# Second norm's rows turned through DRAM, and the linear steps of each window put in another order, in an adaLN transformer block

## The chip, the cores and the metric

The kernel runs on 1 core of one Trainium2 chip, in one launch. The metric is the device time of a run in microseconds (us); less is better. The time of the kernel before is the median of 3 runs.

## The reference

One transformer block with adaptive layer norm (adaLN), on x of 8 batches, 1024 tokens and 512 channels in float32, 16 heads of 32 channels, and an MLP of 2048 hidden channels. Cut to what matters:

```python
mod = silu(condition) @ Wada + bada
sh_a, sc_a, gt_a, sh_m, sc_m, gt_m = split(mod, 6, axis=1)
xn = layernorm(x, g1, be1)                        # over the 512 channels
xm = xn * (1 + sc_a) + sh_a
q, k, v = split_heads(xm @ Wqkv)                  # 16 heads of 32
attn = softmax(causal(q @ k.T * 32 ** -0.5))
x = x + gt_a * ((attn @ v) @ Wproj + bproj)
xn = layernorm(x, g2, be2)                        # the second norm
xm = xn * (1 + sc_m) + sh_m
h = gelu_exact(xm @ W1 + b1)
x = x + gt_m * (h @ W2 + b2)
```

## The kernel before

**Tiles.** The 8 x 1024 tokens are cut into NB = 16 blocks of TB = 512 tokens: `blocks[n]` is (batch, half), so an even n is the first half of a batch and an odd n the second, whose attention also reads the first half's keys and values. P is 128, and a block is four row tiles of 128 tokens by 512 channels (tokens on partitions) or, turned, four chunks of 128 channels by 512 tokens. All matmuls are float32 and split into four tiles of 32 columns (or 32 rows) of the array that run side by side: one call of the helper `matmul` (L201, its instruction is L205) issues four instructions, and the profile counts two records for each of them, so 8 records a call.

**Linear steps.** k, q, v, the attention's projection ("proj"), the four parts of the up matmul ("u") and the down matmul (four parts "d", 7 products in all) are done by Strassen's scheme: 7 products of half-size operands instead of 8. A product of k, q, v, proj or u is 4 calls of `matmul`; a product of d is 16. The operands B11, B21, B22, T1 to T4 are halves of the turned rows (`xm_m`, `xm_a`) and sums of halves (`t_m`, `t_a`), made in `modulated` (L732). Products go to one of three PSUM banks (`banks`), and are combined from there by VectorE (L197) or copied by either VectorE or ScalarE (L189, L192).

**The norms and how rows are turned.** The first norm ("a", of x) and the second ("m", of the residual after the attention) work on rows: statistics (L628) on VectorE, scaling (L653) on ScalarE. Then the rows must be turned so that channels lie on partitions. There are two ways in the kernel. By TensorE: 16 transposes of 128 x 128 a block into PSUM (L769), and the modulation reads PSUM (L778 or L784). Through DRAM (`turn_rows`, L702): VectorE transposes 32 x 32 squares (L708, four instructions a block), four DMAs write them to a DRAM tile ("put", L719), and one DMA reads the turned block back ("get", L725); the modulation then reads and writes SBUF. `is_turned(key)` (L377) picks the way: in the kernel before, DRAM for the first norm of blocks 4 to 15, and TensorE for all others and for every second norm. For the first norm the rows of x are loaded in such an order that the turned columns come out in the order of the tokens.

**The order of the work.** The kernel is laid out by a planner that runs when the program is built. `plan[w]` lists the linear steps of window w; the attention of block w is woven in between. `now` holds a modelled clock for each engine, `due` when an operand is counted as written, and the linear step or the attention's unit that is counted as ready first is written next; what comes out is a fixed order of instructions on each engine. Three lists are worked off beside it: `jobs` (statistics and turns, on VectorE), `pool_jobs`, and `transfers` (the puts and gets). Every DMA but four is issued on SyncE's queue (SP), in the fixed order. Weights come through a ring of 9 tiles (`fetch`, L336); a tile is loaded again when TensorE has used it.

In window w of the kernel before (n = w - 1) the steps are: what is left of the older up and down parts, v(w), the load of the residual's rows (`load_xr`), proj(n), k(w + 1), the second norm's turning `mt`, q(w + 1), up parts, and then down parts of n. The residual of a block (`xr`) has one buffer, block 14 has a buffer of the keys' pool (`kT`, three buffers). The results are stored (L1193) as soon as their last sum has been written into the program. The token half operands of the second norm are contiguous slices: `"B11": xm[:, one, left_half]`.

Of the kernel before, what the change touches and what calls it, by code (L numbers as in the profile page):

```python
# [22 lines left out]
def kernel(  # L23
# [72 lines left out]
    shape = [None]  # L96
    pool_spans = []
    NEVER = float("inf")
# [13 lines left out]
    def note(engine, ns, reads=(), writes=(), port=False):  # L112
        start = max(now[engine], due(reads, writes))
        if port:
            start = max([start] + [b for a, b in pool_spans if a <= start < b])
        end = start + ns
        now[engine] = end
        if engine == "POOL":
            pool_spans.append((start, end))
            del pool_spans[:-16]  # L120
# [80 lines left out]
    def matmul(ps, lhsT, rhs, start, stop, reads=(), bank=None):  # L201

        for j in range(HPG):
            r = slice(j * hd, (j + 1) * hd)
            nc.tensor.matmul(  # L205
                ps[r, :], lhsT[:, r], rhs, start=start, stop=stop, skip_group_check=True
            )
        n = 1
        for d in rhs.shape[1:]:
            n *= d  # L210
        note_pe(2 * COLUMN * n, "columns", reads, [] if bank is None else [("l", bank)])

    MM = 853
# [26 lines left out]
    }  # L240
    late = []
    for w in range(1, NB):
        n = w - 1
        m = mlp_steps(n)
        even = blocks[n][1] == 0
        rows_a = [("rows", blocks[n][0], "a")] if even else []
        rows_m = [("rows", blocks[n][0], "m")] if even else []
        own = m[:1] + ([("load_xa", w + 2)] if w + 2 < NB else []) + m[1:3]
        own += [("norm_a", w + 2)] if w + 2 < NB else []
        if w == NB - 1:  # L250
            steps = late[:1] + [("load_xr", n)] + rows_a + [("proj", n), ("mt", n)] + late[1:]
            steps += [("v", w)] + rows_m + own + m[3:6]
            late = m[6:]
        else:
# [5 lines left out]
            at = [("at", w + 2)] if w + 2 < NB else []  # L260
            if blocks[w][1] == 0:

                late = m[3:4] + at + m[4:]
            else:
                steps += m[3:4] + at + m[4:6]
                late = m[6:]
        plan[w] = steps
    n = NB - 1
    plan[NB] = [("load_xr", n), late[0], ("beside", ("proj", n)), late[1], ("mt", n)] + mlp_steps(n)

# [103 lines left out]

    SQ = 32

    def is_turned(key):  # L377
        return key[0] == "a" and int(key[1:]) >= 4

# [181 lines left out]

    def add_job(job, reads, first=False):

        at = sum(1 for other in jobs if other[2]) if first else len(jobs)
        jobs.insert(at, (job, reads, first))

    def run_jobs(everything=False):
        while jobs and (
            everything or (now["DVE"] <= now["PE"] and due(jobs[0][1]) <= now["PE"])
        ):  # L570
            jobs.pop(0)[0]()

    transfers = []

    def run_transfers(everything=False):
        while transfers and (
            everything or max(queue_free[0], transfers[0][0]) <= now["PE"]
        ):
# [28 lines left out]
    def hurry():  # L607

        while jobs and due(jobs[0][1]) <= now["PE"] + 500:
            jobs.pop(0)[0]()  # L610
        while excursions and due(excursions[0][1]) <= now["PE"] + 500:
            excursions.pop(0)[0]()
# [4 lines left out]
    def normalize(tiles, key, sources):  # L617
# [42 lines left out]
        for t in range(NTT):  # L660
            add_job(lambda t=t: statistics(t), [sources[t]], key[0] == "m")

# [39 lines left out]
    def turn_rows(key, tiles, xm):  # L702

        squares = xm.rearrange("p c (j r) -> p (c j) r", r=P)
        there = kept.tile([D, TB], F32, tag=f"turned_{int(key[1:]) % 2}", name=f"turned_{key}")

        def turn(t):
            nc.vector.transpose(  # L708
                squares[:, :, ts(t, SQ)], tiles[t].rearrange("p (k r) -> p k r", r=SQ)
            )  # L710
# [18 lines left out]
        for t in range(NTT):  # L729
            add_job(lambda t=t: turn(t), [("hat", key, t)])  # L730
# [82 lines left out]
    qTs, kTs, vs = {}, {}, {}  # L813
    projected, valued = set(), set()
    xm_of, hTs, hidden = {}, {}, set()
# [80 lines left out]
    def strassen(step, x, dest, target, row, done, put=None, after={}):  # L896
# [14 lines left out]
        def product(a, t, bank=None):  # L911
            start = bank is None
            reads = [(x, t)] + ([("sums", *step, a)] if raw and a[0] == "S" else [])
            for i in range(2):
                for k in range(2):
# [10 lines left out]
                    lhsT, rhs = (second, first) if row else (first, second)  # L926
                    matmul(
                        banks[bank][:, ts(i, HB)], lhsT[:, ts(i, P)], rhs,
                        start and i + k == 0, k == 1, reads, bank,
# [59 lines left out]
        start(tail())  # L989

    def project_T(step, store, pool, tag, done):

        n = step[1]
        dst = pool.tile([P, NC, TB], F32, tag=tag, name=f"{tag}_{n}")
        store[n] = dst
# [27 lines left out]

    residual, stored = {}, {}
    y_count, y_keys = [0], {}
# [69 lines left out]
    def project_out(n):  # L1095
# [8 lines left out]
        begun = []  # L1104

        def begin(t):

            bank = yield from accumulate(
                [(attT[:, c, ts(t, P)], piece(at[c])) for c in range(NC - 1)], [("att", n)], False
            )  # L1110
            begun.append(bank)

        for t, xt in enumerate(tiles):
            if last:
                while len(begun) <= max(t, 1):
# [3 lines left out]
                matmul(  # L1119
                    banks[bank], attT[:, NC - 1, ts(t, P)], piece(at[NC - 1]), False, True,  # L1120
                    [("att", n, t)], bank,
                )
            else:
                bank = yield from accumulate(
                    [(attT[:, c, ts(t, P)], piece(at[c])) for c in range(NC)], [("att", n)]
                )
# [62 lines left out]
    def store(n, t):  # L1189
        b, h = blocks[n]  # L1190
        for i in (2 * t, 2 * t + 1):
            r0 = h * TB + i * P
            nc.sync.dma_start(out[b, r0 : r0 + P, :], residual[n][:, i, :])  # L1193
        stored[n + 1] = max(stored.get(n + 1, 0.0), due([("xr", n, 2 * t), ("xr", n, 2 * t + 1)]))

    def down(n, part):
# [19 lines left out]
        def product(operand):  # L1216
# [3 lines left out]
            for i in range(NQ):  # L1220
                p = next(at)
                for k in range(2):
                    c = 2 * i + k
                    hT = hTs[n, 2 * kh + c // NC][:, c % NC, tokens]
                    for m in range(2):
# [3 lines left out]
                        else:  # L1229
                            yield [], []  # L1230
                        matmul(
                            banks[bank][:, ts(m, HB)], hT[:, ts(m, P)], halves(p)[:, k, :],
                            c + m == 0, c == 2 * NQ - 1, reads, bank,
# [96 lines left out]
    def perform(step):  # L1330
# [12 lines left out]
        elif kind == "load_xr":  # L1343
            n = step[1]
            b, h = blocks[n]
            if n == NB - 2:
                xr = kvp.tile([P, NTT, D], F32, tag="kT", name=f"xr_{n}")
            else:
                xr = xrp.tile([P, NTT, D], F32, tag="xr", name=f"xr_{n}")
            residual[n] = xr  # L1350
            for t in range(NTT):
                r0 = h * TB + t * P
                nc.sync.dma_start(xr[:, t, :], x[b, r0 : r0 + P, :])
                landed = max(now["PE"], stored.get(n, 0.0)) + LANDING + 700 * t
                written["xr", n, t] = landed
# [15 lines left out]
        elif kind == "k":  # L1371
            yield [("free for k", step[1])], []
            yield from project_T(step, kTs, kvp, "kT", lambda: None)
        elif kind == "q":
# [449 lines left out]
    def attend():  # L1824
        previous = None
        for n in range(NB):
# [20 lines left out]
            written["free for k", n + 2 if n % 2 else n + 1] = 0.0  # L1847
            written["free for k", n + 1] = 0.0
            for g, k, n_slots, upto in slots:
                if (n, g) == groups[-1]:  # L1850
# [50 lines left out]
    def next_scores():  # L1901
        until(lambda: units[unit_at[0]][0] in projected)
        scores(*units[unit_at[0]])
# [15 lines left out]
    needs += sum(score_need(*unit) for unit in units)  # L1919
    for n in range(NB):  # L1920
        written["attended", n] = NEVER
        written["v done", n] = NEVER
# [30 lines left out]
    run_jobs(True)  # L1953
    drain()


# [46 lines left out]
```

## Time and profile before

| what | kernel before |
|---|---|
| median of 3 runs | 3485.6 us (3483.39 to 3485.79) |
| profiled execution, its own time | 3487.44 us |
| its span in the profile | 3485.7 us |
| TensorE (PE) busy | 3448.3 us, 99% |
| VectorE (DVE), ScalarE (ACT), GpSimd (POOL) busy | 1905.0, 1286.7 and 2074.5 us |
| DMA | 466.84 MB, mean 134 GB/s |
| clock granted to TensorE | full speed |

How to read it: busy is the time in which an engine has an instruction; idle time of an engine that is not the bottleneck costs nothing. The profiled execution's own time is 1.7 us longer than its span (launch and end), and 1.8 us longer than the median of the runs. Lines such as L205 are lines of the kernel before; they move by some tens of lines in the changed kernel.

### The profile page before, as it was taken

The numbers are of one execution on the slowest core, as the hardware profiler recorded it, in microseconds if no ns is written. First come the engines' busy times: TensorE is split into PE (matmuls) and PEld (weight loads), VectorE is DVE, ScalarE is ACT, GpSimd is POOL, SyncE is SP. The second block draws the span as 40 slices with busy tenths as digits, with TensorE's granted clock in tenths as the row PEclk, the third lists the DMA queues.
The fourth block names the chain that finished last, engine by engine and source line by source line (L and its number), as shares of the span: only waits on it lengthen the run. The fifth ranks groups of instructions, "written<-read, shape, count | busy, mean of one in ns | idle before, by whom it ended". The sixth has DMA issues, their size and how long they took to land.

```text
span 3485.7 us, 122756 instructions
## 1 busy us (share of the span) xinstructions
PE 3448.3 (99%) x55618; PEld 1776.1 (51%) x55618; DVE 1905.0 (55%) x2136; ACT 1286.7 (37%) x1420; POOL 2074.5 (60%) x2209
## 2 busy tenths in 40 slices
PE   8999999999999999999999999999999999999999
PEld 5544455445554554545545455454554545545445
DVE  6765664554645556465564655645546455554463
ACT  2335243352433524235152352514524244241531
POOL 3676755675466664576645766557664576644640
PEclk9999999999999999999999999999999999999999
DMA  6843334335353353633536335363443534435334
GB/s 213 271 144 86 117 110 150 120 105 172 107 167 102 105 174 104 186 95 100 173 98 186 98 111 159 101 186 98 129 140 101 183 101 135 130 100 153 90 121 136
DMA packets 350523, 466.84 MB, mean 134 GB/s; under 512 B 27460, under 2 KB 212092, under 8 KB 350004
## 3 DMA queue, kind: packets, MB, share of 16 engines
q1 hardware_dynamic: 349808, 458.73, 43.8%
q8 instruction: 438, 7.18, 0.9%
q14 instruction: 81, 0.66, 0.1%
q10 hardware_dynamic: 196, 0.28, 0.0%
HBM read 416.90 MB, written 41.99 MB: 132 GB/s over the span
## 4 chain that ended last, share of the span: by engine, by line
PE 94%; DVE 3%; POOL 1%; ACT 1%; issue 0%; DMA 0%; SPq 0%; DVEq 0%; ACTq 0%; POOLq 0%
PE bank L205 65%; PE sc L1602 9%; PE po L1736 8%; PE st L1695 7%; PE st L1683 3%; DVE mx L1619 2%; PE bank L1757 2%; PE bank L769 1%; PE bank L1657 1%; POOL pT L1821 0%; DVE sc L1616 0%; POOL mcols L1640 0%; DVE pT L1818 0%; POOL mcols L1641 0%; DMA ada<-in_L_cond_Wada_dram 0%
## 5 line engine op out<-in xcount | busy, mean ns | idle before, releaser
L1821 POOL TENSOR_TENSOR pT<-pT,pT 128x256 f32<-128x256 f32 (+3 forms) x1254 | 1174.5, 972 | 210.3 <-ACT pT L1708 119.2
L1708 ACT ACTIVATE pT<-st 128x2048 f32<-128x2048 f32 x288 | 541.1, 1879 | 1001.1 <-PE st L1695 908.8
L205 PE MATMUL bank<-w,hT 128*32 128x256 f32 x14336 | 795.5, 379 | 0.0
L1619 DVE TENSOR_REDUCE mx<-sc 128x4 f32<-128x2048 f32 (+3 forms) x384 | 665.6, 1754 | 140.3 <-PE sc L1602 133.7
L205 PEld LDWEIGHTS bank<-w,hT 128*32 128x32 f32 x14336 | 448.8, 110 | 335.6 <-issue 29.2
L205 PE MATMUL bank<-xm_m,w 128*32 128x256 f32 x8192 | 498.8, 380 | 0.0
L205 PE MATMUL bank<-t_m,w 128*32 128x256 f32 x6144 | 384.2, 380 | 0.1
L205 PEld LDWEIGHTS bank<-xm_m,w 128*32 128x32 f32 x8192 | 253.6, 110 | 238.8 <-issue 76.0
L1713 POOL TENSOR_SCALAR_AFFINE_SELECT pT<-pT 128x512 f32<-128x512 f32 x256 | 164.8, 661 | 308.8 <-ACT pT L1708 306.9
L1602 PE MATMUL sc<-kT,qT 32*128 32x512 f32 (+3 forms) x3072 | 329.1, 520 | 2.9 <-DVE mx L1619 1.9
L1616 DVE TENSOR_TENSOR sc<-sc,mask 128x1024 f32<-128x1024 f32 (+1 forms) x160 | 162.9, 1018 | 276.2 <-PE sc L1602 217.6
L1736 PE MATMUL po<-pT,v 128*32 128x512 f32 (+3 forms) x3072 | 306.0, 493 | 0.0
L1695 PE MATMUL st<-qT,kT 32*128 32x512 f32 (+3 forms) x3072 | 299.8, 486 | 0.0
L205 PEld LDWEIGHTS bank<-t_m,w 128*32 128x32 f32 x6144 | 193.0, 110 | 180.8 <-issue 54.2
L205 PE MATMUL bank<-xm_a,w 128*32 128x256 f32 x3968 | 248.8, 381 | 1.3 <-ACT xm_a L784 1.1
L197 DVE TENSOR_TENSOR hT<-bank,u_u 128x512 f32<-128x512 f32 x192 | 129.1, 686 | 151.2 <-PE bank L205 149.0
L165 POOL TENSOR_TENSOR qT<-top,rec 128x512 f32<-128x512 f32 x60 | 77.1, 1285 | 219.8 <-ACT rec L1775 219.8
L1602 PEld LDWEIGHTS sc<-kT,qT 32*128 32x128 f32 x3072 | 129.4, 183 | 150.9 <-ACT pT L1708 61.8
L205 PE MATMUL bank<-w,qT 128*32 128x256 f32 (+1 forms) x2944 | 191.4, 399 | 1.3 <-DVE qT L1782 1.3
L1153 ACT ACTIVATE hT<-hT,cols 128x512 f32<-128x512 f32 x256 | 164.2, 711 | 55.0 <-DVE hT L197 54.4
L205 PE MATMUL bank<-t_a,w 128*32 128x256 f32 x2944 | 183.3, 380 | 0.0
L165 POOL TENSOR_TENSOR hT<-hT,hT 128x1024 f32<-128x1024 f32 x28 | 79.7, 2868 | 167.6 <-DVE hT L1211 167.6
(232 smaller groups left out, 3507.5 us busy)
## 6 DMA issues: line engine op xcount, KB each, us to landing
w<-in_L_cond_W_dram SPq DMA_DIRECT2D x384, 256.0 KB, 2.9
w<-kept_up_S SPq DMA_DIRECT2D x256, 256.0 KB, 2.6
w<-kept_down_S SPq DMA_DIRECT2D x256, 256.0 KB, 2.8
w<-kept_qkv_S SPq DMA_DIRECT2D x180, 256.0 KB, 2.7
w<-in_L_cond_Wqkv_dram SPq DMA_DIRECT2D x147, 256.0 KB, 3.0
hat<-in_x_dram SPq DMA_DIRECT2D x64, 256.0 KB, 4.7
xr<-in_x_dram SPq DMA_DIRECT2D x64, 256.0 KB, 4.6
out_dram<-xr SPq DMA_DIRECT2D x64, 256.0 KB, 2.6
```

Source lines behind the costliest of these rows:

```text
L165: nc.gpsimd.tensor_tensor(out, a, b, op)
L197: nc.vector.tensor_tensor(out, src, other, op)
L205: nc.tensor.matmul(ps[r, :], lhsT[:, r], rhs, start=start, stop=stop, skip_group_check=True)
L1153: nc.scalar.activation(hT[:, i, :], hT[:, i, :], AF.Gelu, bias=cols[:, O_B1 + f : O_B1 + f + 1])
L1602: nc.tensor.matmul(sc[:, j, c0 : c0 + w], qTs[n][r, gg, ts(qt, P)], keys_of(n, kh)[r, gg, :w], start=True, stop=True, skip_group_check=True,)
L1616: nc.vector.tensor_tensor(place, place, shape_of.to_broadcast(place.shape), ALU.add)
L1619: nc.vector.tensor_reduce(maxima[n, gg][:, kh, qt, :], sc[:, :, c0 : c0 + w], axis=AX.X, op=ALU.max)
L1695: nc.tensor.matmul(st[:, j, c0 : c0 + w], kT[r, gg, ts(k % NTT, P)], qT[r, gg, TB - w :], start=False, stop=True, skip_group_check=True,)
L1708: nc.scalar.activation(pT[:, :, :used], st[:, :, :used], AF.Exp, scale=scale)
L1713: nc.gpsimd.affine_select(diagonal, diagonal, pattern=[[0, HPG], [1, P]], compare_op=ALU.is_ge, fill=0.0, base=0, channel_multiplier=-1,)
L1736: nc.tensor.matmul(po[r, TB - w :], v[:, k % NTT, g * P + j * hd : g * P + (j + 1) * hd], pT[:, j, c0 : c0 + w], start=(k == 0), stop=last ...
L1821: nc.gpsimd.tensor_tensor(into, into, pT[:, j, c0 : c0 + w], ALU.add)
```

## The change

The second norm of blocks 3 to 13 is turned through DRAM, too. For these blocks the residual's rows are loaded, and the results stored, in a permuted order of rows; the turned columns are then in an order in which the token halves are four runs of 64, and `modulated` takes B11, T1, B21 and B22 as strided views. The steps of a window are ordered anew: older up parts, the residual's load, v, proj, `mt`, the four down parts of the block before, q, k, and then the up parts. So a block's down parts run a window later than its up parts, and two residuals are held at a time: odd blocks take a buffer of the keys' pool. Stores become `transfers`, which are issued at the modelled time at which they are counted as ready, as gets are (7000 ns after the last put's issue instead of 5000 ns after the turn). `jobs` are taken in any order across norms. The model now also lets a GpSimd instruction wait for VectorE's use of the shared port.

```diff
     def matmul(ps, lhsT, rhs, start, stop, reads=(), bank=None):
+        if len(rhs.shape) == 3:
+            ps = ps.rearrange("p (a n) -> p a n", a=rhs.shape[1])
...
+    def token_tile(columns, i, n):
+        if is_turned(f"m{n}"):
+            return columns.rearrange("p (a t r) -> p t a r", t=2, r=SQ)[:, i]
+        return columns[:, ts(i, P)]
+    def row_tiles_of(rows, n):
+        if is_turned(f"m{n}"):
+            tiles = rows.rearrange("(h a t r) d -> h t a r d", h=2, t=2, r=SQ)
+            return [tiles[i // 2, i % 2] for i in range(NTT)]
+        return [rows[ts(i, P), :] for i in range(NTT)]
...
-            steps = late + [("v", w), ("load_xr", n)] + rows_a + [("proj", n), ("k", w + 1)]
-            if w == 1:
-                steps = [("load_xr", n)] + rows_a + [("k", w + 1), ("proj", n)]
-            steps += [("mt", n), ("q", w + 1)] + rows_m + own
+        head = rows_a + [("load_xr", n)]
+        if w == 1:
+            steps = head + [("k", w + 1), ("proj", n), ("mt", n), ("q", w + 1)]
+        elif w == 2:
+            steps = downs[2:] + [("v", w)] + head + [("proj", n), ("mt", n), ("q", w + 1), ("k", w + 1)]
+        elif w < NB - 1:
+            steps = late + head + [("v", w), ("proj", n), ("mt", n)] + downs + [("q", w + 1), ("k", w + 1)]
+        else:
+            steps = late + head + [("v", w), ("proj", n), ("mt", n)] + downs
+        cut = m[2] if blocks[w][1] == 0 else None
+        i = ups.index(cut) if cut in ups else len(ups)
+        plan[w] = steps + rows_m + ups[:i]
+        late, downs = ups[i:], m[4:]
...
     def is_turned(key):
-        return key[0] == "a" and int(key[1:]) >= 4
+        n = int(key[1:])
+        return n >= 4 if key[0] == "a" else 3 <= n < NB - 2
...
+    def next_job(by):
+        passed = set()
+        for i, (_, reads, line, _) in enumerate(jobs):
+            if line not in passed and due(reads) <= by:
+                return i
+            passed.add(line)
+        return None
...
     def run_transfers(everything=False):
-        while transfers and (
-            everything or max(queue_free[0], transfers[0][0]) <= now["PE"]
-        ):
-            ready, transfer = transfers.pop(0)
+        while transfers:
+            i = min(range(len(transfers)), key=lambda i: transfers[i][0])
+            if not everything and max(queue_free[0], transfers[i][0]) > now["PE"]:
+                return
+            ready, transfer = transfers.pop(i)
             queue_free[0] = max(queue_free[0], now["PE"], ready) + 700
             transfer()
...
                 for a in range(P // SQ):
                     transfers.append((ready, lambda a=a: put(a)))
-                transfers.append((ready + 5000, get))
         def put(a):
+            if a == P // SQ - 1:
+                transfers.append((queue_free[0] + 7000, get))
...
+        if rows_turned and key[0] == "m":
+            tokens = xm.rearrange("p c (a h n) -> p c h a n", h=2, n=2 * SQ)
+            part["B11"], part["T1"] = tokens[:, one, 0], tokens[:, one, 1]
+            part["B21"], part["B22"] = tokens[:, two, 0], tokens[:, two, 1]
+            for i, t in enumerate(("T2", "T3", "T4")):
+                part[t] = sums[:, i, :, :].rearrange("p c (a n) -> p c a n", n=2 * SQ)
...
     def store(n, t):
-        for i in (2 * t, 2 * t + 1):
-            r0 = h * TB + i * P
-            nc.sync.dma_start(out[b, r0 : r0 + P, :], residual[n][:, i, :])
+        rows = row_tiles_of(out[b, h * TB : (h + 1) * TB, :], n)
+        def move():
+            unstored.remove(n)
+            for i in (2 * t, 2 * t + 1):
+                nc.sync.dma_start(rows[i], residual[n][:, i, :])
+        transfers.append((ready + 1000, move))
...
         elif kind == "load_xr":
-            if n == NB - 2:
-                xr = kvp.tile([P, NTT, D], F32, tag="kT", name=f"xr_{n}")
+            stored_by(n - 2)
+            if n % 2:
+                yield [("free for xr", n)], []
+                spare = key_tag(min(n + 3, NB))
+                xr = kvp.tile([P, NTT, D], F32, tag=spare, name=f"xr_{n}", bufs=1)
```

More of the change, by code (lines that the diff above doesn't have):

```diff
@@ L113, in note @@
         start = max(now[engine], due(reads, writes))
-        if port:
-            start = max([start] + [b for a, b in pool_spans if a <= start < b])
+        if port or engine == "POOL":
+            others = pool_spans if port else port_spans
+            start = max([start] + [b for a, b in others if a <= start < b])
         end = start + ns
         now[engine] = end
-        if engine == "POOL":
-            pool_spans.append((start, end))
-            del pool_spans[:-16]
+        if port or engine == "POOL":
+            spans = port_spans if port else pool_spans
+            spans.append((start, end))
+            del spans[:-16]
         for k in reads:
@@ L1350, in perform @@
             residual[n] = xr
[L1351 to L1354, printed above, removed]
+            for t, rows in enumerate(row_tiles_of(x[b, h * TB : (h + 1) * TB, :], n)):
+                nc.sync.dma_start(xr[:, t, :], rows)
+                landed = max(now["PE"], stored.get(n - 1, 0.0)) + LANDING + 700 * t
                 written["xr", n, t] = landed
@@ L1920 @@
     for n in range(NB):
+        written["free for xr", n] = 0.0 if n == NB - 1 else NEVER
         written["attended", n] = NEVER
@@ L1954 @@
     drain()
+    run_transfers(True)
 _INS = [
```

100 lines of the change are left out of this document (58 added, 42 removed).

## The prediction

> **What bounds the kernel now.** I read the page's busy shares and chain of waits first, then the windows, the groups by form, the timeline of one block, the DMA table and the waits of SyncE's queue.
>
> ```profile
> span 3485.7 us, 122756 instructions
> PE 3448.3 (99%) x55618; PEld 1776.1 (51%) x55618; DVE 1905.0 (55%) x2136; ACT 1286.7 (37%) x1420; POOL 2074.5 (60%) x2209
> PE 94%; DVE 3%; POOL 1%; ACT 1%; issue 0%; DMA 0%; SPq 0%; DVEq 0%; ACTq 0%; POOLq 0%
> PE bank L205 65%; PE sc L1602 9%; PE po L1736 8%; PE st L1695 7%; PE st L1683 3%; DVE mx L1619 2%; PE bank L1757 2%; PE bank L769 1%; PE bank L1657 1%; POOL pT L1821 0%; DVE sc L1616 0%; POOL mcols L1640 0%; DVE pT L1818 0%; POOL mcols L1641 0%; DMA ada<-in_L_cond_Wada_dram 0%
> ```
>
> TensorE is busy 3448.3 of 3485.7 us and is 94% of the chain that ends last; L769, the transposes, is 1% of that chain by itself. Idle time is 37.4 us in all. Where it lies is read from the windows (columns: TensorE, its weight loads, VectorE, ScalarE, GpSimd, clock, DMA):
>
> ```profile
> 0.00:100.00 100.00, 84.18 (x1292) 50.01 (x1296) 64.38 (x94) 29.56 (x40) 36.38 (x55) 0.98 0.62 202
> 1100.00:1200.00 100.00, 99.70 (x1524) 48.55 (x1516) 57.51 (x65) 50.74 (x51) 69.22 (x80) 1.00 0.35 99
> 1200.00:1300.00 100.00, 99.98 (x1754) 55.37 (x1750) 45.46 (x51) 29.71 (x34) 61.43 (x63) 1.00 0.54 162
> 3400.00:3500.00 100.00, 81.25 (x1508) 48.66 (x1500) 33.60 (x44) 10.35 (x16) 6.12 (x3) 0.99 0.39 117
> ```
>
> The first 100 us hold 15.8 us of idle time and the last 85.7 us hold 4.4; in the middle TensorE lacks 0.02 to 0.3 us of 100. So a microsecond of TensorE work taken out of the middle is a microsecond of the time, as long as nothing new makes TensorE wait, and other engines' work is free up to that point.
>
> **Transposes removed.** The two built programs, set side by side, have 304 and 128 instructions on the transposing line: 11 blocks times 16 are gone, 176. Nothing else is gone from TensorE; every other group has its old count. Their price:
>
> ```profile
> L769 PE MATMUL bank<-ident,xh_m 128*128 128x128 f32 x256 | 41.2, 286 | 3.0 <-ACT xm_m L784 2.2 <-ACT xh_m L653 0.7
> 1084.65 1.91 PE L205 MATMUL bank<-xm_a,w 128*32 128x256 f32 x32
> 1086.49 0.40 PE L1683 MATMUL st<-mrow,minus_ones 32*128 32x512 bf16 x4
> 1091.93 1.91 PE L205 MATMUL bank<-t_a,w 128*32 128x256 f32 x32
> 1093.66 1.48 PE L205 MATMUL bank<-xm_a,w 128*32 128x256 f32 x24
> 1100.51 1.48 PE L205 MATMUL bank<-t_a,w 128*32 128x256 f32 x24
> 1101.91 0.66 PE L769 MATMUL bank<-ident,xh_m 128*128 128x128 f32 x4
> 1102.50 0.64 PE L205 MATMUL bank<-t_a,w 128*32 128x256 f32 x8
> 1104.95 0.55 PE L769 MATMUL bank<-ident,xh_m 128*128 128x128 f32 x3
> 1105.43 1.50 PE L205 MATMUL bank<-xm_a,w 128*32 128x256 f32 x24
> ```
>
> Busy time overlaps in a pipelined engine, so I take start to start. Four transposes occupy 1101.91 to 1102.50, 0.59 us, and three 1104.95 to 1105.43, 0.48: 0.11 each, and 0.15 for leaving the whole-array form. 176 x 0.11 = 19.4 us. Entering: 32 matmul records take 1.73 us (1091.93 to 1093.66), 54 ns each; 24 of them are 1.30, and 1100.51 to 1101.91 is 1.40, so entering costs 0.10. The same 0.11 is paid for going from column tiles to row tiles (1084.65 to 1086.49 is 1.84 for 32).
>
> Counted in the two programs' orders, changes of form fall from 1629 to 1583: 44 fewer exits from the transposes (44 x 0.15 = 6.6 us), 28 fewer entries from column tiles (28 x 0.10 = 2.8), but 26 more changes from column to row tiles (26 x 0.11 = 2.9); the other way round I find no cost and take none. Net 6.5 us at most; where a transpose stood at a boundary that was there anyway, the exit replaced one of these, so I take 5. The 3.0 us that TensorE waited before L769 go with 11 of 16 blocks: 2. Sum: 19.4 + 5 + 2 = 26 us less. A bound from below is 19.4 alone, one from above 41.2 x 11/16 + 2 + 5 = 35.
>
> **What is added elsewhere.** 44 square transposes on VectorE, 55 DMAs on SyncE's queue (44 puts, 11 gets, 22 MB in all), and 55 sums that the planner moves from GpSimd to VectorE.
>
> ```profile
> L708 DVE STREAM_TRANSPOSE xm_a<-hat 128x512 f32<-128x512 f32 x48 | 30.8, 683 | 0.0
> L784 ACT ACTIVATE xm_a<-xm_a,shifta,gaina 128x512 f32<-128x512 f32 x48 | 35.2, 804 | 157.8 <-DMA xm_a<-turned_a 128.9 <-DVE y_d L162 17.2 <-DMA w<-kept_down_S 11.7
> L784 ACT ACTIVATE xm_m<-bank,shiftm,gainm 128x512 f32<-128x512 f32 x48 | 36.8, 776 | 47.2 <-PE bank L769 46.4
> turned_a<-xm_a SPq DMA_DIRECT2D x48, 256.0 KB, 4.2
> xm_a<-turned_a SPq DMA_DIRECT2D x12, 1024.0 KB, 5.6
> hat<-in_x_dram SPq DMA_DIRECT2D x64, 256.0 KB, 4.7
> xr<-in_x_dram SPq DMA_DIRECT2D x64, 256.0 KB, 4.6
> L162 DVE TENSOR_TENSOR y<-y,row_ga 128x512 f32<-128x512 f32 x14 | 17.5, 1253 | 0.5
> SPq L725 <- DMA turned_a<-xm_a: 36.5, 17, 3.7
> SPq L1193 <- POOL xr L165: 85.9, 27, 4.5
> ```
>
> VectorE: 44 x 0.683 = 30 us, and 55 sums at the 1.25 of the `y` row make 69; 1905 becomes about 2005 of 3460, 58%, and GpSimd loses as much. Both stay hidden under TensorE. The modulation from SBUF costs ScalarE 804 instead of 776 ns. Permuted row loads cost nothing more: 48 of the 64 `hat` loads are permuted already and land in 4.7 us beside 4.6 for the plain `xr` loads. The same holds for the stores, which nobody but the buffer waits for.
>
> The moved steps take their weights with them through the ring of 9 tiles. In the order of the changed program, each weight's DMA is released at least 10.9 us of TensorE work before its first use, against 11.8 before; they land in under 5 us. What can hold the queue up stands in the last two rows: a get behind its puts 3.7 us at the longest, a store behind GpSimd's sums 4.5. Both are issued later now, when counted as ready, so I cost them at nothing; a hold-up must exceed 10.9 - 4.7 = 6 us to reach TensorE.
>
> **The new wait.** The up parts now wait for DRAM. The timeline of block 4's second norm:
>
> ```profile
> 1065.33 2.37 PE L205 MATMUL bank<-w,qT 128*32 128x256 f32 x40
> 1098.23 2.92 ACT L653 ACTIVATE xh_m<-xr,offset_m,rstd_m 128x512 f32<-128x512 f32 x4
> ```
>
> The projection's last products end at 1067.7 and the scaled rows are done at 1101.15: 33.4 us. Add the turn (4 x 0.683 = 2.7), some 2 for four issues, 7 until the get is issued (longer than the puts' 4.2), 5.6 to its landing, 4 x 0.804 = 3.2 for the modulation and 2 for the first sums: 56 us. What stands between the projection and the first up product in the new order is seven down products of 16 calls, and q and k with seven of 4 calls each: 168 calls x 8 records x 54 ns = 72.6 us, with the attention's units woven in on top. So the round trip is covered with 16 us to spare. In the changed program's order, ten of the eleven gets have 37 to 47 us of TensorE work between their release and the first use; block 5's has 11, against 5.6 + 1.6 for landing and the first two chunks, so up to 4 us may be lost there, once; I take 1. The same count for the first norm's gets: at least 29 us (58 and more before), enough.
>
> TensorE's sum against the profiled span: 3485.7 - 26 + 1 = 3461; with 1.7 us around the span and 1.8 us less for the median of the runs (3485.6 beside 3487.4) the forecast is 3461.
>
> **Rivals.** *Strided operand (slower).* For these blocks four of the seven up products read a moving operand of four runs of 64 elements instead of 256 in one run. No row shows TensorE with such an operand. The nearest rows are those of the second norm's operands, and one line in three lengths:
>
> ```profile
> L205 PE MATMUL bank<-xm_m,w 128*32 128x256 f32 x8192 | 498.8, 380 | 0.0
> L205 PE MATMUL bank<-t_m,w 128*32 128x256 f32 x6144 | 384.2, 380 | 0.1
> L1736 PE MATMUL po<-pT,v 128*32 128x512 f32 x1536 | 202.7, 600 | 0.0
> L1736 PE MATMUL po<-pT,v 128*32 128x256 f32 x512 | 40.0, 385 | 0.0
> L1736 PE MATMUL po<-pT,v 128*32 128x128 f32 x512 | 26.1, 273 | 0.0
> ```
>
> The first row's operands are the strided ones: 8192 x 11/16 = 5632 records, in packs of four that take 4 x 54 = 216 ns, 1408 packs, 304 us. The gain of 25 us is eaten up when a pack takes 18 ns (8%) longer; at 14%, 43 us, the time is 3504. The far upper end is a new start for each run: 600, 385 and 273 ns for 512, 256 and 128 elements leave some 166 ns for a start, three more of them a pack make 0.5 us and 1408 packs 700 us, which would undo the kernel. Below zero nothing is to be had, since the contiguous `xm_m` row goes at the rate of the `t_m` row. I take zero, from those two rows, the nearest in form; the upper end stays outside the range, with a chance of 0.07 for this rival. [...]
>
> *Exposed round trip (a smaller gain).* The planner's clocks decide the order, and ScalarE already sat 128.9 us before the first norm's modulation, mostly at places where it had nothing else to do. If the modulation now holds ScalarE while exponentials queue behind it, TensorE waits for its one score buffer; 1 us a block gives 3472, and from 2.3 us a block on (25/11) nothing is gained. For it: gets among woven attention. Against: 37 us and more from release to use. Chance 0.17, mostly still faster. [...]
>
> *More gain.* The middle of the span holds 37.4 - 15.8 - 4.4 = 17 us of idle time, 2 of which I have counted. Every window has long stretches of linear work without attention; counted in the two orders, those of over 15 us without a unit of the attention come to some 730 us before and 460 after:
>
> ```profile
> 561.27 58.27 PE bank L205 x1080
> 798.84 43.17 PE bank L205 x800
> ```
>
> With the attention spread over more linear work, half of the remaining 15 may go: 3453. Chance 0.13.
>
> **How the numbers follow.** The forecast itself has 0.60 (3456 to 3466), and 0.03 is left for a slowdown of unknown place. The time is 3461; the range runs from 3449 (more gain, or transposes at their upper bound) to 3477 (1.5 us a block exposed), leaving out the strided read and the worst exposures. A measurement can tell about 0.2%, 7 us. Faster by over that: 0.60 + 0.13 + 0.12 of the exposed case = 0.85. Same: 0.04. Slower: the strided read 0.06, the exposed case 0.02, unknown 0.03 = 0.11.
>
> **What would show it.** Right: L769's successor has 80 second-norm transposes instead of 256; TensorE's busy time near 3424 and idle time near 37; mean records of `xm_m` products still 380 ns, start to start 54; turned rows of the second norm landing in 4 to 6 us; VectorE near 58%. Wrong: `xm_m` records longer than `t_m` ones; a new TensorE wait for the modulation or for exponentials of 10 us or more; waits on weights behind puts, gets or stores.

## The result, and the profile after

| what | before | after |
|---|---|---|
| median | 3484.3 us (3483.4 to 3485.8, 5 runs) | 3502.6 us (3500.7 to 3504.0, 5 runs) |
| ratio after/before | | 1.0050 [1.0036, 1.0065] |
| profiled execution, its span | 3487.4, 3485.7 | 3500.8, 3499.0 |
| mean granted clock | 1.000 | 0.997 |

The forecast was 3461; the time rose by 18. The page of the kernel after: busy time, and the chain of waits by engine.

```profile
span 3499.0 us, 122456 instructions
PE 3432.6 (98%) x55442; PEld 1777.6 (51%) x55442; DVE 2045.9 (58%) x2237; ACT 1292.7 (37%) x1432; POOL 2042.8 (58%) x2138
PE 82%; DVE 9%; DMA 4%; ACT 2%; issue 1%; POOL 1%; SPq 0%; DVEq 0%; ACTq 0%; POOLq 0%
```

TensorE has the 176 instructions less (55618 to 55442), but its busy time fell by 15.7 us, not by the 24 forecast (19.4 + 5), and its idle time rose from 37.4 to 66.4. VectorE and DMA, 3% and 0% of the chain before, are now 9% and 4%. The groups by form:

```profile
L210 PE MATMUL bank<-xm_m,w 128*32 128x256 f32 x8192 | 500.7, 381 | 4.2 <-DVE xm_m L818 4.1
L210 PE MATMUL bank<-t_m,w 128*32 128x256 f32 x6144 | 384.2, 381 | 0.1
L809 PE MATMUL bank<-ident,xh_m 128*128 128x128 f32 x80 | 11.9, 283 | 0.8 <-ACT xm_m L824 0.4 <-ACT xh_m L686 0.4
```

The 80 transposes are there as counted, and the strided operand takes 381 ns, as the contiguous `t_m` does. So the gain is there, and something eats it. The waits of TensorE follow (us in total, times, longest). For the softmax, VectorE takes row maxima of the scores `sc` (`mx`), GpSimd writes them into columns (`mcols`), and TensorE turns these and subtracts them in `st`.

```profile
PE st L1750 <- DVE mx L1686: 24.6, 26, 3.6
PE bank L1724 <- POOL mcols L1708: 11.0, 9, 1.6
PE bank L210 <- DVE xm_m L818: 4.1, 1, 4.1
PE bank L210 <- DMA w<-in_L_cond_Wproj_dram: 2.5, 2, 1.5
```

In the kernel before, the wait for `mcols` was 7.3 us, and that for the row maxima was small:

```profile
PE st L1683 <- DVE mx L1619: 2.4, 3, 1.5
```

The windows show where the long ones are (columns as in the prediction; the column after GpSimd is the granted clock):

```profile
1100.00:1200.00 100.00, 96.31 (x1528) 48.76 (x1524) 49.03 (x58) 41.74 (x42) 59.57 (x70) 0.97 0.38 111
1200.00:1300.00 100.00, 98.88 (x1755) 55.16 (x1750) 59.13 (x71) 34.45 (x44) 66.63 (x73) 1.00 0.51 149
1300.00:1400.00 100.00, 95.05 (x1516) 48.67 (x1512) 54.97 (x64) 30.24 (x37) 27.82 (x33) 0.98 0.48 146
1900.00:2000.00 100.00, 96.44 (x1516) 48.03 (x1512) 59.87 (x55) 30.32 (x29) 79.67 (x75) 0.98 0.41 124
2400.00:2500.00 100.00, 96.69 (x1572) 49.85 (x1564) 49.64 (x62) 38.70 (x39) 56.91 (x70) 0.98 0.38 114
2800.00:2900.00 100.00, 96.71 (x1496) 47.37 (x1492) 48.19 (x51) 34.54 (x33) 65.18 (x67) 0.98 0.46 136
```

Five windows lack 3 to 5 us of TensorE each. Each holds one stall of 3.3 to 4.1 us (blocks 4, 5, 8, 10 and 12), and each has a clock of 0.97 or 0.98, unlike the window between them. The timeline of block 4's stall:

```profile
1088.18 1.22 SPq L1253 DMA_DIRECT2D out_dram<-xr  x2
...
1092.09 0.78 SPq L759 DMA_DIRECT2D xm_m<-turned_m  x1
...
1101.35 1.52 ACT L824 ACTIVATE xm_m<-xm_m,shiftm,gainm 128x512 f32<-128x512 f32 x2 [1.93 <-DMA xm_m<-turned_m]
1101.36 2.58 DVE L818 TENSOR_SCALAR xm_m<-xm_m,gainm,shiftm 128x512 f32<-128x512 f32 x2 [4.93 <-issue]
1103.97 1.65 DVE L832 TENSOR_TENSOR xm_m<-xm_m 128x512 f32<-128x512 f32 x1
1105.73 0.69 DVE L834 TENSOR_TENSOR t_m<-xm_m 128x512 f32<-128x512 f32 x1
...
1107.06 0.69 DVE L1683 TENSOR_TENSOR sc<-sc,mask 128x512 f32<-128x512 f32 x1
1107.79 2.29 DVE L1686 TENSOR_REDUCE mx<-sc 128x4 f32<-128x2048 f32 x1
...
1110.14 0.61 PE L1750 MATMUL st<-mrow,minus_ones 32*128 32x512 bf16 x4 [3.64 <-DVE mx L1686]
...
1110.54 1.92 PE L1762 MATMUL st<-qT,kT 32*128 32x512 f32 x8
```

Read it from the bottom. TensorE waits 3.64 us for maxima, and then the next group takes 1.92 us, at a granted clock of 0.50 (1110 to 1116 us), where it takes 1.03 at full clock (kernel before, 1057.21). The maxima are late since VectorE works through its queue in order (they start at 1107.79, when the mask's sum ahead of them has ended), and ahead of them in its queue stand two chunks of the modulation and the first sums. These stood still until 1101.36, when the get issued at 1092.09 had landed (the profile names it at ScalarE's line, and no releaser at VectorE's): 9.3 us, where the planner counts 5 and the prediction took 5.6. The queue that carries the get now waits for loads of the residual, too; such waits came to 1.1 us in the kernel before (SyncE's waits):

```profile
SPq L367 <- DMA xr<-in_x_dram: 39.2, 18, 3.7
```

So two things were to be told apart: why a late get costs so much, and why it is late.

### The profile page after: what moved, and what is told of

Same layout as the page of the kernel before. It is cut to its first block, busy times and chain, and to the rows that moved or that the text cites. A ratio compares the mean times of both kernels' runs of the same rounds, so it can differ in the third digit from the quotient of the medians.

```text
span 3499.0 us, 122456 instructions
## 1 busy us (share of the span) xinstructions
PE 3432.6 (98%) x55442; PEld 1777.6 (51%) x55442; DVE 2045.9 (58%) x2237; ACT 1292.7 (37%) x1432; POOL 2042.8 (58%) x2138
## 4 chain that ended last, share of the span: by engine, by line
PE 82%; DVE 9%; DMA 4%; ACT 2%; issue 1%; POOL 1%; SPq 0%; DVEq 0%; ACTq 0%; POOLq 0%
PE bank L210 56%; PE sc L1669 8%; PE po L1803 7%; PE st L1762 6%; DVE mx L1686 3%; PE st L1750 2%; PE bank L1824 2%; DVE hT L1276 1%; DVE sc L1683 1%; ACT pT L1775 1%; DMA w<-kept_proj_S 1%; DMA w<-in_L_cond_Wproj_dram 1%; DMA xm_m<-turned_m 1%; DMA xr<-in_x_dram 1%; DMA out_dram<-xr 0%
## 5 line engine op out<-in xcount | busy, mean ns | idle before, releaser
L1888 POOL TENSOR_TENSOR pT<-pT,pT 128x256 f32<-128x256 f32 (+3 forms) x1254 | 1220.9, 1009 | 124.1 <-ACT pT L1775 93.9
L210 PE MATMUL bank<-w,hT 128*32 128x256 f32 x14336 | 815.5, 380 | 0.0
L210 PE MATMUL bank<-xm_a,w 128*32 128x256 f32 x3968 | 239.6, 382 | 2.2 <-ACT xm_a L824 1.1
L210 PEld LDWEIGHTS bank<-xm_a,w 128*32 128x32 f32 x3968 | 128.6, 111 | 97.5 <-issue 11.2
```

What stands on the lines that cost most here:

```text
L210: nc.tensor.matmul(ps[r], columns, rhs, start=start, stop=stop, skip_group_check=True)
L1888: nc.gpsimd.tensor_tensor(into, into, pT[:, j, c0 : c0 + w], ALU.add)
```

## The experiments

The theories of the first four expectations: **A**, the get is counted as landed too early, so that its modulation holds VectorE's queue; **B**, the new order of the steps brings the waits by itself. **C** is the strided operand, which the rows above already speak against. **D**, from the fifth run on, says that the get is late because of the shape of the residual's permuted transfers. Ratios are against runs of the kernel before on the same chip, with 95% intervals.

**e1_land12: the get counted as landed later.** Only the planner's figure changes, so the modulation is written behind the maxima.

```diff
-            written["spread", key] = queue_free[0] + 5000
+            written["spread", key] = queue_free[0] + (12000 if key[0] == "m" else 5000)
```

> Edit: the second norm's get is counted as landed 12000 ns after its issue instead of 5000, so its modulation is written later into the engines' orders. Theory A (VectorE is held by a modulation whose get lands 8 to 9 us after its issue, the score maxima queue behind it, TensorE waits 3.3 us at blocks 4, 8, 10 and 12 and loses clock after each): these four waits go (13.5 us) and the half-clock stretches behind them (about 8 us), block 5's wait of 4.1 us may stay: 3480, granted clock 0.999. Theory B (the new order of steps costs the time by itself: late weights at the projection, waits for maxima, more DMA): no change, 3500. Theory C (the strided operand): no change, 3500.

3479.5 us, 0.9981 [0.9972, 0.9991]: 23 us less than the change. TensorE's busy time is 3425.8, the mean clock 1.00, and the wait for the maxima is less than half of what it was:

```profile
PE st L1750 <- DVE mx L1686: 11.2, 23, 1.7
```

A holds: moving the modulation behind the landing takes away the five long stalls and the loss of clock behind them. One stall of 2.8 us, for the projection's weights, remains.

**e2_mod_act: the modulation of turned rows on ScalarE alone.**

```diff
-            on_dve = sooner([held], writes, cost, 780) == "DVE" if turned is None else c % 2
+            on_dve = not rows_turned and sooner([held], writes, cost, 780) == "DVE" if turned is None else c % 2
```

> Edit: every modulation of rows turned through DRAM is put on ScalarE, none on VectorE; nothing else. Theory A: VectorE is free for the maxima, the 3.3 us waits for them go; ScalarE is held instead, and exponentials queue behind it for a part of it: 3480 to 3490. Theories B and C: no change, 3500.

3500.6 us, 1.0042 [1.0027, 1.0057]: a miss (A said 3480 to 3490). VectorE is held all the same, now by the first sum of halves, which needs the modulated chunks (timeline of this kernel, block 4):

```profile
1102.23 1.82 DVE L832 TENSOR_TENSOR xm_m<-xm_m 128x512 f32<-128x512 f32 x1 [5.78 <-ACT xm_m L824]
...
1109.46 0.61 PE L1750 MATMUL st<-mrow,minus_ones 32*128 32x512 bf16 x4 [2.94 <-DVE mx L1686]
```

What counts is when VectorE's queue meets the data of the get (met later, 3479.5 in e1), not which engine modulates (3500.6 here).

**e3_order_only: everything but the turn.** Second norms are turned by TensorE as before, and rows are loaded and stored in their plain order.

```diff
-        return n >= 4 if key[0] == "a" else 3 <= n < NB - 2
+        return n >= 4 if key[0] == "a" else False
```

> Edit: no second norm is turned through DRAM (TensorE transposes all 16 again); the new order of steps, the two residual buffers and the later stores stay. TensorE has the 26 us of transposes again. Theory A: without second-norm gets nobody is held: the 18 us of waits and 10 us of lost clock go, 3502.6 + 26 - 28 = 3500, with TensorE's busy time as before the change, and a granted clock of 1.0. Theory B: the losses stay and the transposes come back: 3528. Theory C: the strided reads go with the turn: under 3490.

3492.1 us, 1.0018 [1.0009, 1.0028]: between A's value and C's, on neither, and far from B's. The change without the turn costs 0.1 to 0.3%. That is the order of the steps together with the rest of the planner's changes (later stores, jobs in any order, the port's model), which no run separates. What the port's model is about shows in the change at VectorE's `mx<-mx` (L1700): 15 of the 32 have no GpSimd sum or mask running beside them and take 0.16 to 0.18 us, the other 17 take 0.47 to 0.87. SyncE's wait for `xr` falls to 0.9 us, and the waits for the maxima are all short:

```profile
PE st L1750 <- DVE mx L1686: 12.7, 20, 1.7
```

So some 6 us are left for B. Adding the turn to this costs another 10 instead of giving 26; A's 23 explain most of these 36, and the rest was open.

**e4_turn_only: the changed kernel with the old plan of the windows.** (`plan[w]` as in the diff's removed lines, the rest as changed.)

> Edit: the second norm of blocks 3 to 13 is turned through DRAM, but the steps stand in the order of the kernel before (k and q between projection and up parts, own down parts after the up parts). Theory A: the gets have only 4 to 17 us of TensorE work before the first use, against 5.4 to 9 us to land and 2 to 3 for the modulation; waits of 0 to 6 us a block with lost clock behind them: 3484 - 26 + 11 x 3 to 8 = 3490 to 3545. Theory B: the order is what costs, so without it the gain shows: 3460. Theory C: 3500.

3737.3 us, 1.0722 [1.0706, 1.0738]: a miss of every theory, by 190 us and more; the run e10 below takes this up.

**e5_wide_both: other shapes for the permuted transfers.** In the built programs the difference stands in the access patterns (stride and count of each dimension, slowest first). A `hat` load, permuted too, has 32 outermost; the changed `xr` loads and stores have 4:

```
before  xr   <- x   [[512, 128], [1, 512]]
after   xr_5 <- x   [[32768, 4], [512, 32], [1, 512]]
```

This run moves the same rows to the same places, in 8 transfers of 32 rows (128 KB) a block and way instead of 4 of 128 rows (256 KB); no engine's order of instructions but the queue's changes. The pieces are smaller, too, but size alone is not the difference: the permuted `hat` loads have 32 outermost at 256 KB and land in 4.7 us in the kernel before. The edit, shortened, for blocks 3 to 13:

```diff
-                nc.sync.dma_start(xr[:, t, :], rows)
+        some = x[b, h*TB:(h+1)*TB, :].rearrange("(h a t r) d -> h a r t d", h=2, t=2, r=SQ)
+        for i in range(2):
+            for a in range(P // SQ):
+                nc.sync.dma_start(xr[a*SQ:(a+1)*SQ, 2*i:2*i+2, :], some[i, a])
```

(Stores likewise, `some[t, a]` from `residual[n][a*SQ:(a+1)*SQ, 2*t:2*t+2, :]`.)

> Edit: the permuted residual loads and the permuted stores of blocks 3 to 13 are cut by groups of 32 rows with these rows outermost (eight transfers of 128 KB a block each way) instead of by row tiles with a dimension of 4 outermost (four of 256 KB); every engine's other instructions and their order stay. Theory D (a transfer with 4 outermost runs on few of the 16 DMA engines, so the loads, the stores and what stands behind them in the queue are late, the gets among them): gets land in 5.5 us everywhere, the 3.3 us waits for maxima shrink under 1 us, the projection's weights come in time, SyncE's 39 us of waiting for loads of the residual go, landing times can be read again: 3470 to 3478, granted clock 0.999 or more. Rival A (the gets are late because 1 MB shares the queue with any stores and weights): no change, 3500.

3476.6 us, 0.9977 [0.9967, 0.9988]: 26 us less than the change, from other shapes for 44 loads and 44 stores (now 88 of each). The longest wait for the maxima is 1.8 us (under 1 was expected), TensorE's busy time 3422.8, the clock 1.00. The DMA table of the kernel after has no landing times, and neither has that of any other kernel here with four-outermost transfers in it:

```profile
xm_m<-turned_m SPq DMA_DIRECT2D x11, 1024.0 KB
```

With these transfers gone they are back (last column: median us from issue to landing):

```profile
xr<-in_x_dram SPq DMA_DIRECT2D x88, 128.0 KB, 4.3
xm_m<-turned_m SPq DMA_DIRECT2D x11, 1024.0 KB, 5.7
out_dram<-xr SPq DMA_DIRECT2D x88, 128.0 KB, 3.1
```

**e6_wide_stores and e11_wide_loads: one way each.**

> Edit: of that, the stores alone. Theory D: the stores stand just before and behind the second norm's gets in the even blocks, so the four waits of 3.3 us shrink; the projection's late weights, which stand behind the loads, stay: 3478 to 3485. Rival A: 3500.

> The changed kernel with the residual's permuted loads alone cut by groups of 32 rows; the stores stay as in the change. With both it took 3476.6, with the stores alone 3484.2, with neither 3502.6. D (stores beside the gets are the larger part, and the two add up): 3492 to 3497. Rival (either alone already frees the queue): 3480 to 3487.

Stores alone: 3484.2, 0.9998 [0.9988, 1.0007]. Loads alone: 3494.9, 1.0030 [1.0019, 1.0041]. That is 18.4 and 7.7 us less than the change, together 26.1, as both at once gave 26.0. The reading is that the stores weigh more because they stand ahead of the gets: in block 4 two are issued at 1088.18, 3.9 us before the get. The waits bear it out: with the loads alone mended, five stalls of 3.3 to 4.4 us stay; with the stores alone, the longest wait for the maxima is 1.7.

**e8_before_perm and e9_before_wide: the shape in the kernel before.** e8 adds to the kernel before nothing but the permuted loads and stores of blocks 3 to 13 and the projection's matching `token_tile`; e9 is e8 with the transfers cut by 32 rows.

> Edit, on the kernel before: blocks 3 to 13 load the residual and store the results in the permuted rows with 4 outermost, and the projection takes its tokens in that order; nothing is turned through DRAM, the order of steps is the old one. The permuted loads' price by itself. Theory D: SyncE waits for the loads, the weights of the projection behind them come late by 1 to 3 us a block: 3490 to 3510. Rival A: permuted rows cost nothing, 3486.

> The kernel before with the permuted order of rows and tokens of blocks 3 to 13, as in the run that took 3538, but its loads and stores are cut by groups of 32 rows (8 of 128 KB each way and block) instead of by fours of rows. D (the shape of the transfers, four long rows outermost, is what costs): 3484 to 3492, about the kernel before, since twice as many issues are on SyncE's queue and nothing else is new. Rival A (the permuted order itself costs, in DRAM or in the projection's token tiles): over 3515.

e8: 3537.6 us, 1.0149 [1.0132, 1.0166]; e9: 3484.8, 1.0000 [0.9991, 1.0009]. The permuted order itself costs nothing, and the shape of its transfers costs 53 us in the kernel before, more than the 5 to 25 expected. The timeline of e8 shows how:

```profile
1036.03 1.70 SPq L1212 DMA_DIRECT2D out_dram<-xr  x2
...
1048.18 2.68 SPq L1371 DMA_DIRECT2D xr<-in_x_dram  x4
1050.91 2.53 SPq L571 DMA_DIRECT2D row_ga<-kept_ga  x1
...
1064.25 0.69 DVE L197 TENSOR_TENSOR y<-bank,row_ga 128x512 f32<-128x512 f32 x1 [8.56 <-DMA row_ga<-kept_ga]
...
1065.00 1.08 PE L206 MATMUL bank<-w,qT 128*32 128x256 f32 x8 [6.49 <-DVE y L197]
```

Two stores are issued by 1037.73; the load into the same buffer waits for them until 1048.18, 10.4 us later (10.2 to 11.2 in the ten blocks where this can be read), and the queue, which had come to this load at 1042.7, stands still for 5.5. In the kernel before these loads wait 0.4 us for stores in all, and a store lands in 2.6 (median):

```profile
out_dram<-xr SPq DMA_DIRECT2D x64, 256.0 KB, 2.6
```

Then the load of the gate's row, a plain one, lands 13.3 us after its issue behind four slow loads; in the kernel before its median is 5.3. The waits of e8, TensorE's and SyncE's:

```profile
PE bank L206 <- DVE y L197: 32.6, 5, 6.7
```

```profile
SPq L1371 <- DMA out_dram<-xr: 54.3, 12, 6.0
```

The trace shows how many of the core's 16 DMA engines are at work, but not for one transfer alone. The next to last column of a window is their mean busy share, and in e8 it stays at 0.24 to 0.29, about 4/16 = 0.25, while hardly anything but these stores and loads is under way:

```profile
1046.00:1048.00 2.00, 2.00 (x35) 0.82 (x24) 0.00 (x0) 0.00 (x0) 0.00 (x0) 1.00 0.29 107
1048.00:1050.00 2.00, 2.00 (x44) 1.18 (x44) 0.35 (x1) 1.79 (x1) 0.00 (x0) 1.00 0.24 90
1050.00:1052.00 2.00, 2.00 (x36) 1.00 (x32) 1.63 (x3) 0.10 (x1) 1.83 (x3) 1.00 0.25 87
```

In the kernel before, the same loads run in 1042 to 1048, and the share is 0.86 to 0.96 there. That a transfer with 4 outermost is carried by four engines is my estimate from these shares; no view shows which engines they are.

**e7_wide_land12 and e12_wide_land8: both remedies.** These are e5 with the get counted as landed after 12 us, and after 8.

> Edit: the transfers of e5 and, as in e1, the second norm's get counted as landed after 12000 ns. Theory D: as e5, and block 5's wait and what is left of ScalarE's and VectorE's holding go: 3466 to 3472. Rival A: as e1, 3479.

> Both permuted transfers cut by groups of 32 rows, and the second norm's gets counted as landed 8 us after their issue instead of 5 (12 in the run that took 3470.5). The gets land in 5.5 to 5.9 us here, so 8 is enough: 3468 to 3473. If the modulation must be further away from the attention's maxima than the landing alone says: 3473 to 3477.

3470.5 us, 0.9958 [0.9943, 0.9973], and 3465.9 us, 0.9943 [0.9929, 0.9958]; e12's median is a little below its range. It has the lowest median of all, 19 us under the kernel before and 37 under the change; its interval overlaps e7's. Set against e3 (3492.1), which differs from it by the turn and the permuted rows that the turn needs, it is 26.2 us faster, with some 5 us to either side by the intervals. So the turn's forecast gain of 26 is there when its gets are neither slow nor waited for too early. Block 4 in it:

```profile
1091.80 0.48 SPq L759 DMA_DIRECT2D xm_m<-turned_m  x1
...
1099.08 2.92 ACT L824 ACTIVATE xm_m<-xm_m,shiftm,gainm 128x512 f32<-128x512 f32 x4
...
1101.36 2.29 DVE L1698 TENSOR_REDUCE mx<-sc 128x4 f32<-128x2048 f32 x1
1104.03 0.40 PE L1762 MATMUL st<-mrow,minus_ones 32*128 32x512 bf16 x4
...
1104.17 0.86 DVE L832 TENSOR_TENSOR xm_m<-xm_m 128x512 f32<-128x512 f32 x1
```

The maxima now stand ahead of the sums in VectorE's queue, the modulation starts without a wait, and TensorE has no stall. Its page and its waits:

```profile
span 3464.5 us, 122643 instructions
PE 3421.6 (99%) x55442; PEld 1777.9 (51%) x55442; DVE 2039.6 (59%) x2236; ACT 1297.0 (37%) x1439; POOL 2032.7 (59%) x2132
```

```profile
PE st L1762 <- DVE mx L1698: 11.5, 25, 1.7
PE bank L1736 <- POOL mcols L1720: 9.8, 8, 1.6
```

**e10_turn_wide: e4 with the transfers cut by 32 rows.**

> The changed kernel with the windows' old order of steps (3737 in that run), its permuted loads and stores cut by groups of 32 rows. D (most of that excess was the slow transfers on one queue, ahead of gets and weights): under 3560. B (in the old order k and q do not cover the round trip of 25 to 30 us a block): 11 blocks at 10 to 20 us, 3600 to 3700.

3698.5 us, 1.0610 [1.0595, 1.0626]. The transfers' shape is worth 39 us here too, and 213 us above the kernel before remain. The number is in B's range, but not its mechanism: TensorE's waits are on maxima (120 us), and those for `xm_m` and `xm_a` come to some 17 us in all.

```profile
PE st L1761 <- DVE mx L1697: 66.3, 27, 10.8
PE bank L1648 <- DVE mx L1667: 53.6, 34, 3.2
PE bank L210 <- DVE xm_a L817: 8.1, 4, 2.6
PE bank L210 <- ACT xm_m L823: 7.2, 3, 4.0
```

At its longest stalls, three of 10.77 us, VectorE works off the residual's sums, in turn with GpSimd, and then turns the squares of a first norm before it comes to the maxima. There the old order of steps loses by the order in which the planner then fills VectorE's queue; for the other waits this is open. Against the kernel before, idle time is up by 147 us, and busy time by 67 although the transposes are gone, at a clock of 0.976. The total of 213 is not broken down further, and why the old order costs so much stays open.

## Why the prediction was wrong

**What held.** The transposes' price: TensorE's busy time is 3422.8 in e5 and 3421.6 in e12, beside 3448.3, a fall of 25.5 and 26.7 where 24 of busy time was forecast; TensorE's wait before the transposes fell from 3.0 to 0.8, by the 2 forecast. The strided operand costs nothing (381 ns against 381), so that rival is refuted. VectorE came to 58%, with 2046 us busy where 2005 were summed. The permuted order costs nothing by itself (e9: 1.0000).

**What came out by luck.** Block 5's wait was 4.1 us, and the prediction says "up to 4 us may be lost there". But its working does not give that: 11 us of TensorE work against 5.6 + 1.6 leaves 4 us to spare and loses none. The wait came from a get that took 10.9 us to its use (1319.68 to 1330.60) where 5.6 was taken, and in e5 TensorE does not wait for these rows.

**Two readings that were loose.** That "in the middle TensorE lacks 0.02 to 0.3 us of 100" holds for the two windows shown; between 400 and 3300 us it is 0 to 1.04. And the range's lower end, 3449, lies below what its two grounds give (3453 for more gain, 3452 for the upper bound of the transposes). Neither bears on the miss.

**The step that failed.** "Permuted row loads cost nothing more: 48 of the 64 `hat` loads are permuted already and land in 4.7 us ... The same holds for the stores". The row was right and did not apply: the `hat` loads are permuted with 32 outermost, the new transfers with 4. I compared what the transfers do to the rows, and not the pattern that the instruction carries. Their price is 26 us in the changed kernel (e5), and 53 in the kernel before (e8 against e9). The sentence on the stores, "which nobody but the buffer waits for", forgot what the next paragraph counts for the moved weights: one queue carries them all, and a get that is issued 3.9 us behind two slow stores lands late (9.3 us after its issue in block 4). That paragraph looks for hold-ups of the queue at the gets and the stores and costs them "at nothing"; the queue's 39.2 us of waiting for `xr` is not among them.

**The mechanism that was named and priced too low.** The exposed round trip was to show as "the modulation now holds ScalarE while exponentials queue behind it", 1 us a block, mostly still faster. It came on VectorE, in five of eleven blocks: in four as a wait of 3.3 to 3.6 us for the maxima, in block 5 as one of 4.1 for the modulated rows themselves. ScalarE's place was argued from the trace of before, where the modulation of turned rows was its work; the planner is free to give chunks to VectorE, and the sums after them are VectorE's anyway (e2). The "37 us and more from release to use" counted TensorE's use of the rows only; VectorE's queue meets them before they have landed, 9 us after the get's issue, with a unit's maxima behind. This step and the one above are not two separate losses: a later modulation alone gives 23 us (e1), fast transfers alone 26 (e5), both together 32 to 37 (e7, e12).

**What was not in the sum at all: the clock.** Against e12, the change has 23.5 us more of idle time and 11.0 us more of busy time for the same instructions. The latter lies behind the stalls, where the granted clock falls to 0.50. In block 4 it is 0.66 in 1109 to 1110 us, 0.50 from 1110 to 1116 and 0.92 in the microsecond after; eight records of scores take 1.92 us there instead of 1.03. Behind each of the other four stalls, 1.7 of 4 us are missing from the clock. Summed over windows of 1 and 2 us, 10.2 us of full clock are missing behind the five, about the 11.0. Shorter stalls are not safe: four windows of e2, in which TensorE is idle for 2.7 to 3.2 us in all and no wait for maxima is over 2.9, have 0.98. How long a stall must be to cost clock was not shown.

**The rest of the distance to the forecast.** e12's span is 3464.5, the forecast's 3461. Idle time is 42.9 there beside 37.4: maxima +9.1 and `mcols` +2.5, against some 2 less before the transposes and some 4 less in small ones. The waits for the maxima come with the rest of the change: e3, without the turn, has 12.7 and is 6 us slower than the kernel before. The prediction moved the steps at no cost, looking only at their weights; and the "More gain" from spreading the attention did not come.

## What to carry over

Before a transfer is called as cheap as another, compare the access patterns of the two as the program carries them: the size of the outermost dimension above all, which was worth 26 us here (4 against 32, e5) and 53 in the kernel before (e8 against e9). A wait on a DMA is to be costed on the in-order queue that meets it first, with whatever is written behind it; in a planner, a landing time that is counted too short writes the waiting instruction ahead of urgent ones, and one figure (5 to 8 or 12 us) was worth 11 and 6 us even with fast transfers, 23 with slow ones. And a stall of TensorE near 3 us can cost more than its length, here about 2 us of clock for each of five.

## What the runs showed of the hardware

- Stores of 256 KB from 128 partitions to DRAM with 4 x 32 rows as their two outermost dimensions take about four times as long as those with 128 outermost: in e8 the buffer is released 10.4 us after the issue of the last of them, in the kernel before a store lands in 2.6 (median). While such stores and loads run nearly alone, 0.24 to 0.29 of the core's 16 DMA engines are busy (e8, 1046 to 1052 us). A plain transfer issued behind them on the same queue is late with them (a gate's row 13.3 us in e8, instead of a median of 5.3 before). Cut in two of 128 KB with 32 outermost, they land in 2.9 to 5.1 us (medians of stores and loads in e5, e7, e9 and e12).
- TensorE's granted clock was 0.50 behind each of the change's five stalls of 3.3 to 4.1 us, for about 6.8 us in block 4 and about 3.4 in the other four; windows of 100 us with one such stall had 0.97 or 0.98. In e2 four windows with waits of up to 2.9 us had 0.98, and the one of block 5's stall, 5.1 us, 0.95. In the kernel before, a stall of 2.1 us that ended at 23.9 us was followed by 0.50 (26 to 28 us). Behind its other stalls from 20 us on, of up to 1.7 us, the change had 1.00, as e5 had in four windows with waits of up to 1.8.
- Float32 moving operands in runs of 64 elements go through TensorE as fast as contiguous ones do: 381 ns a record in the change's `xm_m` row, as in its `t_m` row.
